# One index copy for four scatters in a graph network on one core

## The chip, the cores and the metric

The kernel runs on one core of a Trainium2 chip. The metric is device time in microseconds (us) of one execution, and lower is better. The five engines are TensorE (PE in the profile, with its weight loads as PEld), VectorE (DVE), ScalarE (ACT), GpSimd (POOL) and SyncE (SP). Each runs its own instructions in the order in which the program wrote them, and they wait for one another through semaphores.

## The reference

A graph of 12,500 nodes with 64 features and 200,000 edges, sorted by destination, goes through two blocks. The first block is a layernorm, a ReLU and two SAGE convolutions; the second is a layernorm, a ReLU and a message layer over the edges. Cut to what matters:

```python
def _sage_conv(x, src, dst, Wl, Wr, b):
    agg = jax.ops.segment_sum(x[src], dst, num_segments=N)
    cnt = jax.ops.segment_sum(jnp.ones((src.shape[0],), x.dtype), dst, num_segments=N)
    mean = agg / jnp.maximum(cnt, 1.0)[:, None]
    return mean @ Wl.T + b + x @ Wr.T
...
h = jnp.maximum(_layernorm(x, axis=-1), 0.0)
h = jax.nn.relu(_sage_conv(h, src, dst, W1l, W1r, b1))
x = x + _sage_conv(h, src, dst, W2l, W2r, b2)
h = jnp.maximum(_layernorm(x, axis=-1), 0.0)
inp = jnp.concatenate([h[src], h[dst], edge_attr_64], axis=-1)
msg = jax.nn.relu(inp @ W1 + b1) @ W2 + b2
x = x + _segment_mean(msg, src, N)
```

The part of `inp @ W1` that belongs to `edge_attr_64` needs neither convolution. The kernel calls its 200,000 rows of 64 the edge terms, and works them out early.

## The kernel before, in words

The nodes are cut into 49 blocks of 256. A cell is a pair of a source block and a destination block. There are 49 x 49 = 2401 cells, and each cell has 128 slots for its edges. Gathers and sums over edges are matmuls with one-hot matrices, cell by cell, so that edges have to be brought into the order of cells and slots.

**The sort.** The generator `sort(B)` handles the edges whose destination lies in block B: at most 34 columns of 128 edges. Among other things it works out, for each of them, the row that it has in a table in memory, and writes these rows as integers into `pos[:, B]`, a tile of 128 x 40 x 34 for the blocks below `EARLY` = 40 (line 651). The last nine blocks have theirs in `pos_late`. The operations of the sort (lines 589 to 666) are spread over the first convolution.

**The convolutions.** `some_cells` gathers four cells at a time (line 896, into PSUM tiles `got`), ScalarE copies them out (line 900), VectorE makes the one-hot matrix `hot` (line 750), and three turns later TensorE adds the cells up with it (line 775). The one-hot matrices of the gather, `turned` (line 741), are made by VectorE from source rows that SyncE loads (line 731). The main loop (lines 947 to 961) goes over all cells in groups of four, for layer 0 and then for layer 1. In each turn it emits `some_cells`, in layer 0 some steps of the sort and of the clearing of the tables, one half of the next `turned`, and then the work beside.

**The work beside.** `edge_terms` is a generator, and `Beside.passed` lets it go one step for every 4.45 units of due time, where a cell counts 1.1 in layer 0 and 0.9 in layer 1. For each group of four blocks it goes through their 17 pairs of columns, three at a time. A unit is one pair of columns of four neighbouring blocks. TensorE transposes the four (line 399), ScalarE copies them (line 405), TensorE multiplies them by the weights (line 414), and ScalarE copies the result into `terms_o`, which has three buffers (line 422). Then `scatter` sends the unit's 4 x 2 pieces of 128 rows to their places in memory, each by an indirect DMA that GpSimd issues. There are 170 such units in the convolutions, so 1360 scatters. The last nine blocks follow in the message stage with units of three and 306 scatters.

**One scatter.** For each half h of the pair and each block of the unit, VectorE copies one column of `pos` (128 rows by one integer) into a small tile `turn_i` of its own, of which there are 16 buffers (lines 380 and 381). GpSimd then issues the DMA that reads its 128 row numbers from that tile (line 382). After each scatter the generator yields. Of a unit's eight scatters, six go out one by one in the next unit's steps, and the rest at the end of those steps. A buffer of `turn_i` can be written again when the DMA that read from it has landed. GpSimd's scatters take eight DMA semaphores in turn.

**The order.** The program is emitted by hand in this order; VectorE's queue holds the copies between `hot`, `turned` and the operations of the sort. The messages come after both convolutions and read the edge terms back (line 1130).

Of the kernel before, what the change touches and what calls it, by code (L numbers as in the profile page):

```python
# [11 lines left out]
I32 = mybir.dt.int32  # L12
# [3 lines left out]
P = 128  # L16
# [98 lines left out]
def fast_path(  # L115
# [19 lines left out]
    nc = tc.nc  # L135
# [27 lines left out]
    EARLY = J * BJ * HALVES  # L163
# [7 lines left out]
    def table_of(B):  # L171

        if B < EARLY:
            q, i = divmod(B // J, BJ)
            return q * J + B % J, BJ, i
        i, j = divmod(B - EARLY, LJ)
        return HALVES * J + j, len(range(j, LATE, LJ)), i
# [78 lines left out]
    for n, b in enumerate((b1, b2, lb1, lb2)):  # L256
        t = consts.tile([P, D], FT, name=f"bias{n}")
# [97 lines left out]
    def edge_terms(work, psum, groups, ITEMS, U):  # L355


        loads = []
        for blocks in groups:
            step = ITEMS // len(blocks)  # L360
            loads += [(blocks, t0, min(step, TG - t0)) for t0 in range(0, TG, step)]

        def load(blocks, t0, m):
            n = len(blocks)
            e = work.tile([P, ITEMS, 2 * D], FT, name="edges")
            for i, B in enumerate(blocks):
                s = nc.sync.value_load(begin_i[0:1, B:B + 1], min_val=0, max_val=E - WIN)
                a = edge[bass.ds(s, WIN)].rearrange("(p t) d -> p t d", t=T)
                nc.sync.dma_start(e[:, i * m:(i + 1) * m].rearrange("p c d -> p (c d)"),
                                  a[:, 2 * t0:2 * (t0 + m)].rearrange("p t d -> p (t d)"))  # L370
            return e

        def scatter(o, unit):
            for h in range(2):
                for c, (B, tg, _) in enumerate(unit):
                    assert sorted_blocks() > B
                    t = 2 * tg + h
                    j, n, _ = table_of(B)
                    assert j in cleared
                    at = work.tile([P, 1], I32, name="turn_i", bufs=16)  # L380
                    nc.vector.tensor_copy(at, pos_of(B)[:, t:t + 1])
                    nc.gpsimd.indirect_dma_start(  # L382
                        out=terms[j][:], out_offset=bass.IndirectOffsetOnAxis(ap=at, axis=0),
                        in_=o[:, c, h], in_offset=None,
                        bounds_check=S * NB * n - 1, oob_is_err=False)
                    yield


        before = iter(())
        ahead = load(*loads[0])  # L390
        for at, (blocks, t0, m) in enumerate(loads):
            e = ahead
            items = [(B, t0 + c, e[:, i * m + c]) for c in range(m) for i, B in enumerate(blocks)]
            units = [items[u:u + U] for u in range(0, len(items), U)]
            for u, unit in enumerate(units):
                k = len(unit)
                pt = psum.tile([P, 4, P], FT, name="pE")
                for c, (_, _, a) in enumerate(unit):
                    nc.tensor.transpose(pt[:, c], a, ident)  # L399
                if u == 0 and at + 1 < len(loads):  # L400
                    ahead = load(*loads[at + 1])
                next(before, None)
                yield
                et = work.tile([P, U, P], FT, name="edges_t", bufs=2 if U == 4 else 1)
                nc.scalar.copy(et[:, :k], pt[:, :k])
                next(before, None)
                yield
                next(before, None)
                if U == 4:
                    next(before, None)  # L410
                yield
                pm = psum.tile([P, 4, 2, D], FT, name="pE")
                for c in range(k):
                    nc.tensor.matmul(pm[:, c], et[:, c], we, start=True, stop=True)  # L414
                next(before, None)
                yield
                next(before, None)
                yield
                for _ in before:
                    pass  # L420
                o = work.tile([P, U, 2, D], FT, name="terms_o", bufs=3)
                nc.scalar.copy(o[:, :k], pm[:, :k])
                before = scatter(o, unit)
                yield
        for _ in before:
            pass
# [72 lines left out]
    pos = terms_work.tile([P, EARLY, T], I32, name="pos", bufs=1)  # L499

    def pos_of(B):
        return pos[:, B] if B < EARLY else pos_late[:, B - EARLY]
# [196 lines left out]
    def sorted_blocks():  # L699
        return sorted_to[0] // STEPS  # L700
# [106 lines left out]
    work = layers.enter_context(tc.tile_pool(name="layers", bufs=2))  # L807
# [169 lines left out]
    work = ctx.enter_context(tc.tile_pool(name="last", bufs=2))  # L977
# [450 lines left out]
```

## Time and profile before

| what | us |
|---|---|
| median of three runs | 3727.71 |
| lowest and highest of them | 3725.05, 3731.02 |
| the profiled execution's own time | 3723.96 |
| its span, from the first to the last instruction | 3722.1 |
| features, first sort, set-up | 0 to about 200 |
| first convolution | about 200 to 1290 |
| second convolution | about 1290 to 2300 |
| messages, with the late blocks' edge terms | about 2300 to 3400 |
| messages of the late blocks, end | about 3400 to 3722 |

The granted TensorE clock is 0.991 over the span. In the profile a group of instructions is named by its line, its engine, its operation and the tiles that it writes and reads; then come its count, its busy time, the mean time of one in ns, and the idle time of its engine just before, with what ended it. "L382 POOL DMA_INDIRECT terms<-terms_o,turn_i" is thus the scatter on GpSimd, and "L381 DVE COPY turn_i<-pos" the copy of one column. Busy time counts what is covered by at least one instruction of the engine. The chain is followed from the last instruction back to what released each step.

### The profile page before, as it was taken

The page shows a single profiled execution, that of the slowest core. Times are in us where ns is not written, and L with a number is a line of the kernel's source. Part 1 is how long each engine was busy: PE and PEld are TensorE (multiplying, and loading weights), DVE is VectorE, ACT ScalarE, POOL GpSimd, SP SyncE. Part 2 cuts the span into 40 slices and gives each one's busy share as a digit, 9 for nine tenths or more (in the row PEclk, how much of TensorE's full clock was granted, in tenths as well). Part 3 has the DMA queues.
Part 4 walks back from the last instruction along what each step waited for, and adds up shares of the span by engine and source line. Part 5 has one row for each costly group of instructions (what it writes and reads, how often), then busy time and mean ns, then how long its engine had stood idle before and what let it go on. Part 6 is the DMA issues. An engine that isn't in the chain of part 4 may idle for free.

```text
span 3722.1 us, 130679 instructions
## 1 busy us (share of the span) xinstructions
PE 3505.5 (94%) x51318; PEld 3423.2 (92%) x51318; DVE 3322.8 (89%) x7346; ACT 2568.7 (69%) x5875; POOL 2732.6 (73%) x2306
## 2 busy tenths in 40 slices
PE   1799999999999999999999998999999999998987
PEld 0799999999999999999999998899999999998887
DVE  7899999999999978888888887899999999998998
ACT  3466666666666667777777776688888888876665
POOL 4057787777778777777777774688888888996454
PEclk9999999999999999999999999999999999999999
DMA  6654555555454344444444444666666666666664
GB/s 209 247 169 148 159 153 157 156 157 156 137 166 151 116 129 141 136 136 144 136 131 140 139 132 131 227 215 203 217 214 212 203 216 210 208 196 193 196 213 138
DMA packets 413697, 635.90 MB, mean 171 GB/s; under 512 B 94131, under 2 KB 296247, under 8 KB 413070
## 3 DMA queue, kind: packets, MB, share of 16 engines
q1 hardware_dynamic: 353106, 572.87, 48.7%
q0 software_dynamic: 53312, 51.36, 4.6%
q8 instruction: 402, 6.59, 0.7%
q10 hardware_dynamic: 6652, 3.24, 0.4%
q14 instruction: 225, 1.84, 0.2%
HBM read 474.72 MB, written 155.83 MB: 169 GB/s over the span
## 4 chain that ended last, share of the span: by engine, by line
PE 75%; DVE 15%; DMA 4%; issue 3%; ACT 2%; POOL 1%; SPq 1%; DVEq 0%; POOLq 0%; ACTq 0%
PE acc L775 26%; PE got L896 17%; PE got L1077 11%; PE got L1078 6%; PE pE L414 4%; DVE hot L750 3%; DVE turned L741 2%; PE pE L399 2%; DVE hot_r L635 2%; PE pX L645 2%; DVE turned_d L741 1%; DMA terms_in<-terms 1%; PE acc L839 1%; PE got L1074 1%; PE pX L617 1%
## 5 line engine op out<-in xcount | busy, mean ns | idle before, releaser
L382 POOL DMA_INDIRECT terms<-terms_o,turn_i x1666 | 1937.7, 1163 | 663.3 <-issue 220.5
L900 ACT CAST rows<-got 128x384 bf16<-128x384 f32 x2402 | 1038.5, 487 | 592.3 <-PE got L896 577.7
L775 PEld LDWEIGHTS <-hot 128*128 128x128 bf16 x12006 | 1029.5, 98 | 19.0 <-issue 7.9
L775 PE MATMUL acc<-rows,hot 128*128 128x193 bf16 x9604 | 1006.0, 247 | 0.7 <-DVE hot L750 0.7
L1089 POOL TENSOR_TENSOR hidden<-hidden 128x512 f32<-128x512 f32 (+1 forms) x602 | 756.3, 1257 | 259.6 <-ACT hidden L1086 179.3
L896 PEld LDWEIGHTS <-turned 128*128 128x128 bf16 x9604 | 814.7, 98 | 67.4 <-issue 27.5
L750 DVE TENSOR_TENSOR hot<-dcol,local 128x1024 bf16<-128x1024 bf16 x1202 | 814.3, 682 | 4.1 <-PE acc L775 3.7
L741 DVE TENSOR_SCALAR turned<-srow,nid 128x2048 bf16<-128x2048 bf16 (+1 forms) x906 | 780.4, 875 | 21.1 <-issue 10.7
L1077 PE MATMUL got<-ta,turned 128*128 128x128 bf16 x3920 | 599.8, 220 | 7.3 <-DVE turned L741 7.3
L1077 PE MATMUL got<-tb,turned_d 128*128 128x128 bf16 x3920 | 600.7, 221 | 1.7 <-DVE turned_d L741 1.1
L1078 PE MATMUL got<-tb,turned_d 128*128 128x64 bf16 x3920 | 546.9, 193 | 0.0
L1078 PE MATMUL got<-ta,turned 128*128 128x64 bf16 x3920 | 546.5, 193 | 0.0
L896 PE MATMUL got<-ta,turned 128*128 128x192 bf16 x4802 | 499.7, 247 | 37.4 <-issue 24.8
L1097 ACT ACTIVATE hot_a<-every,scol 128x256 bf16<-128x256 bf16 x1200 | 507.0, 493 | 0.0
L896 PE MATMUL got<-tb,turned 128*128 128x192 bf16 x4802 | 494.1, 246 | 0.8 <-DVE turned L741 0.5
L1086 ACT ACTIVATE hidden<-y 128x512 f32<-128x512 f32 (+1 forms) x301 | 190.4, 632 | 293.5 <-DVE y L1083 169.5
L1077 PEld LDWEIGHTS <-turned 128*128 128x128 bf16 x3920 | 362.8, 98 | 8.2 <-issue 7.8
L1077 PEld LDWEIGHTS <-turned_d 128*128 128x128 bf16 x3920 | 360.2, 98 | 2.9 <-DVE turned_d L741 2.4
L1078 PEld LDWEIGHTS <-turned 128*128 128x128 bf16 x3920 | 359.5, 98 | 1.2
L1078 PEld LDWEIGHTS <-turned_d 128*128 128x128 bf16 x3920 | 359.9, 98 | 0.0
L741 DVE TENSOR_SCALAR turned_d<-drow,nid 128x2048 bf16<-128x2048 bf16 (+2 forms) x302 | 324.9, 1117 | 0.0
L1099 ACT ACTIVATE hot_a<-hot_a 128x1024 bf16<-128x1024 bf16 x300 | 317.2, 1057 | 9.5
(227 smaller groups left out, 5302.4 us busy)
## 6 DMA issues: line engine op xcount, KB each, us to landing
srow<-srow_b SPq DMA_DIRECT2D x300, 512.0 KB
srow<-srow_k SPq DMA_DIRECT2D x149, 512.0 KB
drow<-drow_k SPq DMA_DIRECT2D x149, 512.0 KB
terms_in<-terms SPq DMA_DIRECT2D x294, 160.0 KB
edges<-in_edge_attr_dram SPq DMA_DIRECT2D x200, 192.0 KB
terms<-tb SPq DMA_DIRECT2D x200, 160.0 KB
terms<-tb SPq DMA_DIRECT2D x48, 640.0 KB
terms<-terms_o,turn_i POOLq DMA_INDIRECT x1666
```

Of the source, the lines that this page charges most:

```text
L382: nc.gpsimd.indirect_dma_start(out=terms[j][:], out_offset=bass.IndirectOffsetOnAxis(ap=at, axis=0), in_=o[:, c, h], in_offset=None, bound ...
L741: nc.vector.tensor_scalar(o[:, h, :n * S], r[:, :n * S], nid[:, h:h + 1], None, op0=OP.is_equal)
L750: nc.vector.tensor_tensor(o[:, :n], cols.rearrange("p (g c) -> p g c", c=2).unsqueeze(2).to_broadcast([P, n, 2 * P, 2]), local.rearrange(" ...
L775: nc.tensor.matmul(self.acc[B][:, h, :W3], lt, r[:, c, 0:W3], start=k + h == 0, stop=k == row - 1 and h == 1, skip_group_check=True)
L896: nc.tensor.matmul(p[:, (i - c) * D3:(i - c + 1) * D3], t[:, h, (a - c0 + i) * S:(a - c0 + i + 1) * S], table[:, (a + i) % NB, h], start=h ...
L900: nc.scalar.copy(g[:, c:c + m, :D3], p[:, :m * D3].rearrange("p (c d) -> p c d", c=m))
L1077: nc.tensor.matmul(p[:, c], lt, rt[:, 0:2 * D], start=i == 0, stop=False, skip_group_check=True)
L1078: nc.tensor.matmul(p[:, c, 0:D], lt, rt[:, 2 * D:], start=False, stop=i == 3, skip_group_check=True)
L1086: nc.scalar.activation(w[:, :n, 0:D], y[:, :n], AF.Relu)
L1089: nc.gpsimd.tensor_sub(w[:, :n, (i + 1) * D:(i + 2) * D], w[:, :n, j], upper(w)[:, :n, j])
L1097: nc.scalar.activation(q[:, c - k], every, AF.Abs, scale=-1.0, bias=scol[:, scol_at[last] + a + c:scol_at[last] + a + c + 1])
L1099: nc.scalar.activation(q[:, :n - k], q[:, :n - k], AF.Relu, bias=1.0, scale=-2.0)
```

## The change

For blocks below 40, `scatter` makes one tile of 128 x 4 for each half of the unit, with four buffers, and fills it with one VectorE copy. The copy takes the same column of the four neighbouring blocks, so its source has a stride of 34 integers. It stands just before the first of the four scatters, and the four scatters each take one column of it. The late blocks keep one copy for each scatter. An assertion says that the unit's blocks are neighbours with the same pair of columns.

```diff
         def scatter(o, unit):
             for h in range(2):
-                for c, (B, tg, _) in enumerate(unit):
+                B0, t = unit[0][0], 2 * unit[0][1] + h
+                assert [(B, tg) for B, tg, _ in unit] == [(B0 + c, unit[0][1]) for c in range(len(unit))]
+                if B0 < EARLY:
+                    four = work.tile([P, len(unit)], I32, name="turn_i", bufs=4)
+                    nc.vector.tensor_copy(four, pos[:, B0:B0 + len(unit), t])
+                for c, (B, _, _) in enumerate(unit):
                     assert sorted_blocks() > B
-                    t = 2 * tg + h
                     j, n, _ = table_of(B)
                     assert j in cleared
-                    at = work.tile([P, 1], I32, name="turn_i", bufs=16)
-                    nc.vector.tensor_copy(at, pos_of(B)[:, t:t + 1])
+                    if B0 < EARLY:
+                        at = four[:, c:c + 1]
+                    else:
+                        at = work.tile([P, 1], I32, name="turn_i", bufs=16)
+                        nc.vector.tensor_copy(at, pos_of(B)[:, t:t + 1])
                     nc.gpsimd.indirect_dma_start(
                         out=terms[j][:], out_offset=bass.IndirectOffsetOnAxis(ap=at, axis=0),
                         in_=o[:, c, h], in_offset=None,
```

## The prediction

> **What bounds the kernel now.** I read the page's busy shares and chain first, then the busy time by stage, then the chain and the waits of each convolution alone, then the timeline around the copies. The page:
>
> ```profile
> PE 3505.5 (94%) x51318; PEld 3423.2 (92%) x51318; DVE 3322.8 (89%) x7346; ACT 2568.7 (69%) x5875; POOL 2732.6 (73%) x2306
> PE 75%; DVE 15%; DMA 4%; issue 3%; ACT 2%; POOL 1%; SPq 1%; DVEq 0%; POOLq 0%; ACTq 0%
> ```
>
> TensorE sets the time over three quarters of the chain, VectorE over 15%. Those 15% are not spread evenly. Busy time by stretch (window, length, busy us and instructions of PE, PEld, DVE, ACT and POOL, granted clock, DMA share, GB/s; the rows are the first convolution, the second, and the first part of the message stage):
>
> ```profile
> 200.00:1290.00 1090.00, 1048.16 (x12357) 1006.99 (x12356) 1020.61 (x2608) 696.65 (x1746) 846.13 (x685) 1.00 0.50 151
> 1290.00:2300.00 1010.00, 1008.60 (x11463) 996.41 (x11461) 843.71 (x2453) 727.82 (x1956) 752.38 (x676) 1.00 0.44 137
> 2400.00:3300.00 900.00, 899.17 (x16903) 896.43 (x16901) 842.52 (x1297) 725.72 (x1366) 805.01 (x678) 1.00 0.67 210
> ```
>
> In the second convolution TensorE is busy for 1008.6 of 1010 us; its chain, added up, is 1005.2 us TensorE and 1.1 us VectorE, and no index copy stands on it. Nothing taken from VectorE there can shorten it. In the first convolution the sort runs beside the gather, VectorE is busy for 1020.6 of 1090 us, and the chain's pieces add up to 679.7 us TensorE, 327.1 VectorE, 33.5 ScalarE, 23.4 DMA, 22.9 issue. Only here can the change pay.
>
> Who waits there (window 200 to 1290; total us, times, longest):
>
> ```profile
> POOL terms L382 <- DVE turn_i L381: 49.6, 121, 3.0
> ...
> PE pX L645 <- DVE hot_r L635: 11.3, 15, 1.9
> ...
> PE got L896 <- DVE turn_i L381: 8.2, 8, 2.2
> ...
> PE pX L598 <- DVE hot L594: 5.5, 5, 1.5
> ...
> PE pX L598 <- DVE turn_i L381: 4.0, 6, 1.2
> ```
>
> When TensorE waits for VectorE, it is for about 0.9 us at a time (29.0 us in 34 waits by the four lines of PE). A wait named after turn_i is one for an operation that ended beside a copy, since TensorE reads no index.
>
> **The copies removed.** The scatter helper makes 1360 copies of one column for blocks below 40 (692 start in the first convolution, 668 in the second) and 306 for the late blocks, which keep theirs. The row of the first convolution, and one stretch of the timeline (start, us):
>
> ```profile
> L381 DVE COPY turn_i<-pos 128x1 int32<-128x1 int32 x692 | 86.9, 146 | 0.0
> ```
>
> ```profile
> 408.87 0.19 DVE L650 SCALAR_TENSOR_TENSOR pos_f<-rank,kv 128x34 f32<-128x34 f32 x1
> 409.09 0.18 DVE L651 TENSOR_SCALAR pos<-pos_f 128x34 int32<-128x34 f32 x1
> 409.18 0.75 DVE L741 TENSOR_SCALAR turned<-srow,nid 128x2048 bf16<-128x2048 bf16 x1
> 409.85 0.21 DVE L381 COPY turn_i<-pos 128x1 int32<-128x1 int32 x2
> 409.97 0.68 DVE L750 TENSOR_TENSOR hot<-dcol,local 128x1024 bf16<-128x1024 bf16 x1
> 410.57 0.15 DVE L381 COPY turn_i<-pos 128x1 int32<-128x1 int32 x1
> 410.63 0.68 DVE L750 TENSOR_TENSOR hot<-dcol,local 128x1024 bf16<-128x1024 bf16 x1
> ```
>
> A copy lasts 146 ns but the next operation starts 0.06 us after it: neighbours overlap. From start to next start the 692 copies take 43.4 us, 63 ns each, and that is what the stream gains. So 146 ns would overstate it 2.3 times. Of those 43.4 us, 11.3 us stand on the chain of the first convolution (about 26%, near VectorE's own share of the chain, 30%).
>
> **The copy of four that is added.** The trace has none. Lower bound: 63 ns, a one-column copy. Upper: the 128x34 write of pos (line 651), whose next operation starts about 94 ns after it. Four columns against 34 lie near the lower end: 63 + 3/33 of 31 = 66 ns. On the chain 11.3 us become 11.3 x 66 / (4 x 63) = 3.0 us (4.2 by the upper bound): **8.3 us** less, 7.1 at worst. In the second convolution 668 copies become 167, some 31 us of VectorE's time, hidden beside TensorE's 1008.6; if TensorE were not full there, that would count as well.
>
> [...]
>
> **The wait that is added.** Every copy but the first 16 waits on one DMA semaphore: buffer n is free when scatter n-16 has landed. A tile of four is free when all four of its scatters have, and it is asked for at the first of the next four. So scatter n-13 must have landed, not n-16, and one copy waits on four semaphores. That is up to two more semaphore instructions in VectorE's queue:
>
> ```profile
> L841 DVEq EVENT_SEMAPHORE  x98: 21/21/21, 155.1 to 2312.3; - x98
> L1081 DVEq EVENT_SEMAPHORE  x541: 21/50/4106, 2333.5 to 3697.6; - x181
> ```
>
> They run while the operation before them is still busy, mostly 0.6 us or more (a hot or a turned), so I take nothing. Uncovered, a pair costs about 0.1 us (two of line 1081 start 98 ns apart): 173 groups x 0.26 on the chain x 0.1 = 4.5 us.
>
> What queues behind a copy that waits is the next hot, and behind that TensorE's accumulation (line 775). How near is that wait? GpSimd is nearly full (window 200 to 1290):
>
> ```profile
> L382 POOL DMA_INDIRECT terms<-terms_o,turn_i x685 | 846.7, 1236 | 355.4 <-DMA terms<-tb 120.6 <-issue 90.5 <-DVE turn_i L381 49.6
> ```
>
> 1236 ns and a regular 0.305 us between two scatters; from 360 to 1290 us only 31 of 590 waited longer than that. Its lag behind the copies grows from 4.6 us (median of the first hundred) to 15.0 (of the eighth). I took each landing as the last increment of the scatter's semaphore before the semaphore's reuse eight scatters later, 2.1 to 6.4 us after the start. Against these, the copy of four would have had to spare in the first convolution: median 9 us, 5% under 3.7, least 0.3 (at 998 us), and 3.6 to 7 in its last 55 us. So no stall as the timing stands. At 1304 to 1430 us 13 groups would stall, 18.4 us together, 3.5 at most. That is in the second convolution, where hot runs 5 us ahead of TensorE at 1300 us and some 31 ahead from 1400: covered. Uncovered, it would be up to 18 us.
>
> But a first convolution that runs x us faster brings its copies x us nearer to GpSimd's scatters, and GpSimd does not speed up. Some 5 us are to be had before the end's slack (3.6 to 7) is gone, and the dip near 860 to 1000 us (about 3 us) takes a little on the way. **Sum**: 8.3 off the chain, some 3 given back to that wait: 5 us. Ends: 8.3 off and nothing off.
>
> On the profiled execution's 3723.96 us (span 3722.1 and 1.9 around it) that gives 3719; against the median of the runs, 3727.71, it gives **3722.7**. What a measurement here can tell from no change is about 0.2%, 7.5 us; the forecast lies inside it.
>
> **Rivals.** *The whole gain comes through.* For it: TensorE's waits for VectorE are 0.9 us each, while a VectorE stretch of the chain (38 stretches, 4.6 copies each) loses only 0.2 us, so VectorE mostly stays last. Against it: GpSimd's lag. With ScalarE's, DMA's and issue's pieces counted as VectorE's too (407 us at the copies' 4.0%, three quarters of it) it is 12 us: 3716; by the chain alone 3719.4. I put 3718 for it and count it as faster.
>
> *GpSimd becomes the bound.* Place: scatters of the first convolution, through the shorter ring of index buffers. Scatters with no copy in their first 966 ns lasted 1291 ns on average, with one 1183, with two 1147. If the copies are what lets GpSimd in, going from 0.6 to 0.16 copies a scatter makes it about 1274: 38 ns x 685 = 26 us later by 1290, less the 4 us of slack: 22 us, 3750. It decides from about 6 ns a scatter (4 us over 685). Against it: a long VectorE operation explains both the long scatter and the missing copy, and removing copies leaves the long operations' total as it is.
>
> [...]
>
> *It does nothing*: the semaphore instructions (4.5 us) and the ring take all: 3727.7.
>
> **How the numbers follow.** Forecast, 2 to 7 us off: 0.36, its own range 3720 to 3726. Nothing: 0.11. Whole gain: 0.33. GpSimd: 0.20. So faster 0.33, within 0.2% 0.47, slower 0.20. The range goes from the 12 us of the first rival with 3 us of scatter between runs, 3713, to 3737, 9 us slower: GpSimd 13 us later at the end of the first convolution, less its 4 us of slack. That leaves out perhaps 5% below and 14% above.
>
> **What would show it.** Copies: 340 of 128x4 and 306 of one column; VectorE busy in 200 to 1290 down by some 30 us. Right: the second convolution keeps its length and the first loses about 5. The step on the ring: idle of VectorE before the copy, by a DMA, near the end of the first convolution and in the 130 us after it, and none on TensorE behind the latter. The step on scatters: mean within 10 ns of 1236. Wrong: a mean of 1260 or more, a first convolution over 1090, or a second one that changes.

## The result: slower by a seventh of a per cent, and the profile after

The changed kernel takes 3732.96 us (median of 20 runs, 3723.93 to 3739.97); the kernel before, in 20 runs, 3727.75 (3719.49 to 3734.19). The ratio is 1.0014, with a 95% interval from 1.0008 to 1.0020. So it is 5 us slower, where 5 us faster was forecast. The time lies inside the stated range, but on the other side of the kernel before. The profiled execution took 3731.2 us, with a span of 3729.3, 7.2 us more than that of before.

The page after, busy shares and chain:

```profile
PE 3502.5 (94%) x51318; PEld 3419.9 (92%) x51318; DVE 3270.4 (88%) x6326; ACT 2568.9 (69%) x5875; POOL 2750.9 (74%) x2306
PE 74%; DVE 13%; DMA 5%; issue 4%; POOL 2%; ACT 1%; SPq 1%; DVEq 0%; POOLq 0%; ACTq 0%
```

VectorE has its 1020 instructions fewer and 52 us less busy time. On the chain VectorE has lost 2 points; DMA and GpSimd have won one each. The two convolutions (same windows and columns as before; the first really ends near 1340 us, where the first gather of the second starts):

```profile
200.00:1290.00 1090.00, 1041.07 (x12232) 999.27 (x12230) 986.81 (x2066) 690.08 (x1731) 859.00 (x678) 0.99 0.49 150
1290.00:2300.00 1010.00, 1008.56 (x11466) 996.24 (x11464) 816.78 (x1951) 726.39 (x1949) 756.48 (x683) 1.00 0.43 135
```

In the first window VectorE is busy for 34 us less, and yet TensorE did 125 matmuls fewer in it: the work is later. GpSimd did 7 scatters fewer and was busy 13 us longer. The start of the same gather matmul, read off both traces, tells where the time went (us):

| gather matmul | before | after | difference |
|---|---|---|---|
| 300 | 189.6 | 188.9 | -0.7 |
| 1500 | 498.1 | 495.0 | -3.1 |
| 2400 | 730.1 | 731.0 | +0.9 |
| 3000 | 883.3 | 890.8 | +7.6 |
| 4200 | 1197.8 | 1203.5 | +5.7 |
| 4800, the end of the first convolution | 1338.3 | 1348.5 | +10.2 |
| 9600, the end of the second convolution | 2304.1 | 2314.6 | +10.5 |

In this pair of traces the change wins 2.4 us between 190 and 500 us, loses 13 between 500 and 1340, and is neutral in the second convolution; 3 us come back in the message stage. What VectorE waited for in the window 200 to 1290 after the change, where before no copy waited at all:

```profile
DVE ranks L632 <- ACT ranks L625: 30.9, 30, 2.3
DVE turn_i L379 <- DMA terms<-terms_o,turn_i: 26.1, 25, 3.4
```

One such wait in the chain (start, us, what; window 705 to 732):

```profile
707.21 0.29 DVE both L830
707.80 0.97 POOL terms L389
...
717.96 1.67 POOL terms L389
...
721.32 6.99 DMA terms<-terms_o,turn_i
728.60 0.60 DVE hot L757
```

Read it downwards. The chain leaves VectorE, runs through a row of scatters on GpSimd and the landing of one of them, and comes back to VectorE's `hot`, which had been queued behind a copy of four. In the window 200 to 1290 the chain's pieces add up to 50.9 us on GpSimd's scatters and 72.0 us on their DMAs; before, they were 2.8 and 11.9. And the scatters themselves (same window):

```profile
L389 POOL DMA_INDIRECT terms<-terms_o,turn_i x678 | 859.4, 1268 | 342.2 <-issue 162.8 <-DMA terms<-tb 119.5 <-DMA terms<-terms_o,turn_i 19.0
```

They last 1268 ns on average instead of 1236. Nothing in the change touches the scatter, except that its index stands in a column of four.

### The profile page after: what moved, and what is told of

The parts are those of the page before. It is cut to its first block, busy times and chain, and to the rows that moved or that the text cites. A ratio compares the mean times of both kernels' runs of the same rounds, so it can differ in the third digit from the quotient of the medians.

```text
span 3729.3 us, 129317 instructions
## 1 busy us (share of the span) xinstructions
PE 3502.5 (94%) x51318; PEld 3419.9 (92%) x51318; DVE 3270.4 (88%) x6326; ACT 2568.9 (69%) x5875; POOL 2750.9 (74%) x2306
## 4 chain that ended last, share of the span: by engine, by line
PE 74%; DVE 13%; DMA 5%; issue 4%; POOL 2%; ACT 1%; SPq 1%; DVEq 0%; POOLq 0%; ACTq 0%
PE acc L782 26%; PE got L903 17%; PE got L1084 11%; PE got L1085 6%; PE pE L421 4%; DMA terms<-terms_o,turn_i 2%; PE pE L406 2%; PE pX L652 2%; DVE turned L748 2%; DVE hot L757 2%; DVE hot_r L642 2%; DVE turned_d L748 1%; POOL terms L389 1%; PE got L1081 1%; PE acc L846 1%
## 5 line engine op out<-in xcount | busy, mean ns | idle before, releaser
L1096 POOL TENSOR_TENSOR hidden<-hidden 128x512 f32<-128x512 f32 (+1 forms) x602 | 756.1, 1256 | 255.9 <-ACT hidden L1093 174.3
```

The costliest lines, as they stand in the source:

```text
L1096: nc.gpsimd.tensor_sub(w[:, :n, (i + 1) * D:(i + 2) * D], w[:, :n, j], upper(w)[:, :n, j])
```

## The experiments

Three theories stood at the start. RING: the index tiles now come free in fours, so VectorE waits. GPSIMD: the scatters became slower and GpSimd is the bound. SEMAPHORES: the 672 added semaphore instructions cost. Ratios are to the kernel before on the same chip.

**A first set, not comparable.** On its chip the kernel before itself took 4267 us (3724 to 3728 elsewhere), so its four kernels say nothing about 5 us. The granted clock of these runs of before was 0.95 to 0.96.

`e1`: eight tiles of four instead of four.

```diff
-four = work.tile([P, len(unit)], I32, name="turn_i", bufs=4)
+four = work.tile([P, len(unit)], I32, name="turn_i", bufs=8)
```

> The changed kernel with eight tiles of four instead of four, so that a copy waits for scatter n-29 instead of n-13; 340 copies and 672 semaphore instructions as in the change. Theory RING (the shorter ring of index tiles makes VectorE wait for landings, 26 us in the first convolution): these waits go to zero, the chain there loses its pieces on GpSimd and DMA (123 us), and the time is 3719 to 3725, below the 3727.8 of before. Theory GPSIMD (scatters last longer because the removed copies were openings for GpSimd, 1268 ns on average against 1236, and it is the bound whatever the ring): the waits leave the copies and come back at ScalarE's write of terms_o, which has three buffers; the time stays at 3730 to 3734. Theory SEMAPHORES (the added semaphore instructions cost): no change from 3733.

`e2`: the kernel before with 13 buffers.

```diff
-at = work.tile([P, 1], I32, name="turn_i", bufs=16)
+at = work.tile([P, 1], I32, name="turn_i", bufs=13 if B < EARLY else 16)
```

> The kernel before, with its own copy for each scatter, and 13 buffers for them in the convolutions instead of 16: only the ring is shortened, to what the first copy of four sees. RING: copies wait for landings, 5 to 25 us of VectorE idle in the first convolution, and the time is 3731 to 3741. GPSIMD: all copies are there, so scatters last 1236 ns and the time is 3728. SEMAPHORES: none is added, 3728.

`e3`: the change with idle one-column copies.

```diff
 at = four[:, c:c + 1]
+if c:
+    spare = work.tile([P, 1], I32, name="spare_i", bufs=16)
+    nc.vector.tensor_copy(spare, pos[:, B, t:t + 1])
```

> The changed kernel, and beside the second, third and fourth scatter of each half a one-column copy into a tile that nobody reads: VectorE's stream is as long as before the change, the ring is that of the change. RING: the saving is undone and the waits stay, 3734 to 3742. GPSIMD: the openings are back, the mean scatter of the first convolution falls from 1268 to about 1236 ns and the time returns to 3726 to 3730. SEMAPHORES: 3734 to 3742 as RING, with no fewer waits than the change if it is the semaphores that are late.

`e4`: the kernel before with 28 buffers.

```diff
-at = work.tile([P, 1], I32, name="turn_i", bufs=16)
+at = work.tile([P, 1], I32, name="turn_i", bufs=28 if B < EARLY else 16)
```

> The kernel before with 28 buffers for its copies instead of 16. No copy waited before, so RING, GPSIMD and SEMAPHORES all expect 3726 to 3730; if it is faster than that by more than 2 us, sixteen were already too few.

Measured there: e1 1.0384 (1.0354 to 1.0415), e2 1.0002 (0.9973 to 1.0030), e3 1.0329 (1.0294 to 1.0365), e4 1.0008 (0.9988 to 1.0028). Both kernels with a copy of four lost over 3% there, with and without idle copies. No such loss appeared in any other run of the change, and its cause stays open: the clock there is 3 to 4% lower, the time of the kernel before 14% longer. For 28 buffers this is the only run; it agrees with sixteen having been enough.

**The same again, at the usual pace.**

`f1`: eight tiles of four, as e1.

> The same kernel as e1_four_ring8 (eight tiles of four, a copy waits for scatter n-29), taken again because the first convolutions of that call, of the kernel before too, ran at another pace than in the runs that the question is about. RING: no copy waits for a landing, the first convolution is as long as before the change or shorter, the time is 0.9977 to 0.9995 of before. GPSIMD: the wait comes back at ScalarE's write of terms_o, 1.0005 to 1.002. SEMAPHORES: 672 semaphore instructions as in the change, 1.001 to 1.002.

Measured: 0.9999 (0.9990 to 1.0008). What ScalarE and TensorE waited for in the first convolution:

```profile
ACT terms_o L429 <- DMA terms<-terms_o,turn_i: 14.2, 8, 4.5
...
PEld pE L406 <- ACT terms_o L429: 9.9, 5, 3.8
```

The copies no longer wait, and the loss of the change is gone. The gain does not come, though; the result lies between the forecasts of RING and GPSIMD. The wait has moved to the next buffer in line, `terms_o`, whose three buffers come free when the scatters of three units back have landed; the scatters last 1273 ns. (The execution that was profiled took 3731.0 us, 6 above the median of its kernel, so these waits may be longer than usual.) RING is right about which wait costs the 5 us, and GPSIMD about what stands behind it. SEMAPHORES falls: at the two to a copy of the change, 664 semaphore instructions are there (the first eight copies need none), and nothing is lost.

`f2`: the kernel before with 13 buffers, as e2.

> The same kernel as e2_before_ring13 (the kernel before with 13 buffers). RING: some copies wait for landings in the first convolution, 5 to 25 us, 1.0005 to 1.003 of before. GPSIMD and SEMAPHORES: 1.000.

Measured: 1.0005 (0.9996 to 1.0014), scatters 1245 ns. The trace has one wait of 0.3 us at a copy up to 1290 us, and eight between 1304 and 1350, 12.2 us together and 3.1 at most. The second convolution does not cover these: TensorE's first gather in it, near 1340 us, waits until VectorE has got past them. That wait before, and in f2:

```profile
PE got L896 <- DVE bad_t L965: 0.3, 1, 0.3
PE got L896 <- DVE bad_t L965: 4.5, 1, 4.5
```

`bad_t` names the operation with which VectorE ended just before the gather began. From gather matmul 4800 to 4900 f2 loses 5.5 us against the trace of before. So the shorter ring alone can cost 4 to 5 us at this one place. The time shows neither that it does as a rule nor that it does not: the interval reaches from 0.9996 to 1.0014. (f2 is also a little stricter than the change: each of its copies waits for the scatter 13 back, in the change only one in four.)

`f3`: the change with idle copies, as e3.

> The same kernel as e3_four_idle_copies (the change, with three one-column copies that nobody reads beside each copy of four). RING: 1.002 to 1.004 of before, copies wait as in the change or more. GPSIMD: mean scatter of the first convolution back to 1236 ns, 1.000. SEMAPHORES: 1.002 to 1.004.

Measured: 1.0000 (0.9991 to 1.0009). Its scatters in the first convolution:

```profile
L392 POOL DMA_INDIRECT terms<-terms_o,turn_i x686 | 847.7, 1236 | 354.8 <-issue 166.5 <-DMA terms<-tb 120.5 <-DMA terms<-terms_o,turn_i 18.5
```

With 1020 useless copies put back, the scatters last 1236 ns again, although their index still stands in a column of four; no copy waits with the short ring, and the loss is gone. RING alone expected 1.002 and more. So the loss of the change goes away with a longer ring (f1) and with faster scatters (f3): it is made by slower scatters and a ring too short to ride over them. What the ring costs without the slower scatters stays open (f2).

`f4`: one copy of eight columns for a unit, four tiles.

```diff
-if B0 < EARLY:
-    four = work.tile([P, len(unit)], I32, name="turn_i", bufs=4)
-    nc.vector.tensor_copy(four, pos[:, B0:B0 + len(unit), t])
+if B0 < EARLY and h == 0:
+    eight = work.tile([P, len(unit), 2], I32, name="turn_i", bufs=4)
+    nc.vector.tensor_copy(eight, pos[:, B0:B0 + len(unit), t:t + 2])
```

> One copy of eight columns (both halves) for a unit's eight scatters, with four tiles of eight: the copy waits for scatter n-25, and there are 170 copies with eight semaphores to wait for instead of 340 with four. RING: no waits at the copies, and another 12 us less in VectorE's stream: 0.997 to 0.9995 of before. GPSIMD: 1.0005 to 1.002. SEMAPHORES: the number of semaphore instructions stays near 672, 1.001 to 1.002.

Measured: 1.0042 (1.0028 to 1.0055), outside what all three expected. The first convolution:

```profile
ACT terms_o L429 <- DMA terms<-terms_o,turn_i: 36.7, 20, 6.2
...
PEld pE L406 <- ACT terms_o L429: 27.1, 17, 5.7
```

```profile
L389 POOL DMA_INDIRECT terms<-terms_o,turn_i x668 | 861.6, 1290 | 340.8 <-issue 177.6 <-DMA terms<-tb 125.9 <-DMA terms<-terms_o,turn_i 14.7
```

Fewer VectorE instructions still, slower scatters still, a longer wait at `terms_o`. No copy waits for more than 0.2 us up to 1290 us. So the slower scatters cost time with the ring out of the way too, through `terms_o`.

**Who paces whom.**

`g1`: the change with another pace of the edge terms.

```diff
-beside.passed((z - a) * (1.1, 0.9)[layer])
+beside.passed((z - a) * (1.06, 0.93)[layer])
```

> The changed kernel with the edge terms paced at 1.06 a cell in the first convolution and 0.93 in the second, instead of 1.1 and 0.9: scatters fall due every 1.61 us in the first instead of 1.55, and every 1.45 in the second instead of 1.50. OPENINGS (without the copies a scatter lasts 1.27 us and 0.305 follow, so GpSimd falls behind and is what the first convolution ends up waiting for): at 1.61 GpSimd keeps up, the waits at the copies fall from 26 us to under 5, and what the copies saved on VectorE shows: 0.997 to 0.999 of before. RING: waits fall as well, by less; 0.999 to 1.001. If neither holds and the copies of four cost something of their own: 1.001 as the change.

Measured: 0.9987 (0.9978 to 0.9996). No copy waits up to 1290 us, with scatters of 1288 ns, but one waits for 2.7 us at 1330, just before the first gather of the second convolution, and TensorE with it:

```profile
PE got L903 <- DVE bad_t L972: 1.7, 1, 1.7
```

`g2`: the kernel before with that pace.

> The kernel before with the same pace, 1.06 and 0.93. OPENINGS and RING: no copy waited before, so nothing is won, 0.9990 to 1.0005; GpSimd's lag no longer grows in the first convolution. If the pace by itself pays (fewer matmuls and copies of the edge terms in the crowded convolution), 0.997 to 0.999, and the gain of g1_four_pace is not the change's.

Measured: 0.9989 (0.9980 to 0.9998). The pace pays by itself, so g1's gain is not the change's; with GpSimd given 4% more time, change and kernel before are equal within the noise. In the traces g1 is 2.7 us ahead of g2 at gather matmul 4800 and 0.5 us behind at 4900, across that one wait. So even here the ring takes the gain back; OPENINGS, which expected it to show, missed that.

`g3`: as f3, with memsets for idle operations.

```diff
-nc.vector.tensor_copy(spare, pos[:, B, t:t + 1])
+nc.vector.memset(spare, 0)
```

> As f3_four_idle_copies, but the three idle operations beside each copy of four are memsets of 128x1, which read nothing. OPENINGS, if any short operation lets GpSimd in: the first 300 scatters last 1.21 to 1.24 us as with idle copies, against 1.27 to 1.31 without, and the time is 1.000. If a copy's reading or its longer pass is what counts: 1.26 us and more, 1.001 to 1.002.

Measured: 0.9977 (0.9968 to 0.9986), faster than the kernel before. Scatters of the first convolution:

```profile
L392 POOL DMA_INDIRECT terms<-terms_o,turn_i x695 | 825.2, 1187 | 376.2 <-issue 171.3 <-DMA terms<-tb 120.2 <-DMA terms<-terms_o,turn_i 21.6
```

The scatters are 81 ns shorter than after the change, by operations that do nothing. That beats the expectation, which was 1.000. No copy waits in this trace. The memsets add little to VectorE's stream (some 8 ns each in h1 below), so it is the scatters that took the waits away, and not a VectorE that comes later.

`g4`: the kernel before with every copy made twice.

```diff
 nc.vector.tensor_copy(at, pos_of(B)[:, t:t + 1])
+if B < EARLY:
+    spare = work.tile([P, 1], I32, name="spare_i", bufs=4)
+    nc.vector.tensor_copy(spare, pos[:, B, t:t + 1])
```

> The kernel before with a second, idle copy beside each of the 1360 copies: the dose the other way. OPENINGS: scatters of the first convolution fall from 1236 ns to about 1180 to 1210, and GpSimd's lag there no longer grows; VectorE's stream is 43 us longer there, of which 11 stand on the chain, so 1.001 to 1.004. If scatters last as long as VectorE is busy and copies play no part: 1236 ns or more, 1.003 to 1.006.

Measured: 1.0063 (1.0049 to 1.0077), scatters 1277 ns instead of the 1180 to 1210 of the theory. So "each copy is an opening for GpSimd" is too simple: one copy in a place shortens scatters (f3: 1268 to 1236 ns), two in the same place lengthen them (1236 to 1277). The other theory on record, that scatters last as long as VectorE is busy, expected 1236 ns or more and 1.003 to 1.006 and comes near; but after the change VectorE is busy for less and the scatters last longer, which contradicts it.

**The disputed cost by itself.**

`h1`: scatters beside VectorE in thirteen rhythms.

```python
for name in SECTIONS:
    ...
    for k in range(K):
        nc.gpsimd.indirect_dma_start(
            out=table[:], out_offset=bass.IndirectOffsetOnAxis(ap=at[:, k:k + 1], axis=0),
            in_=rows, in_offset=None, bounds_check=P * K - 1, oob_is_err=False)
    ...
    for n in range(150):
        if kind == "hot" or kind == "mix" and n % 3:
            hot()
        else:
            turned()
        for m in more:
            small[m]()
```

> Nothing of the network is computed; the output holds x. Thirteen stretches, in each 40 scatters of 128 rows beside VectorE, which is idle, or runs hot alone, turned alone, or two hots and one turned in turn, plain or with one short operation after each: a copy of 128x1, two of them, a memset of 128x1, a copy of 128x4 from columns 34 apart. [...] If short operations play no part: all stretches beside hot alike within 20 ns.

Measured, by stretch (40 scatters each; busy us, mean ns):

```profile
L81 POOL DMA_INDIRECT terms_mix<-terms_o,turn_i x40 | 71.3, 1784 | 58.1 <-DMA terms_mix<-terms_o,turn_i 56.4 <-DVE turn_i L79 1.8
...
L81 POOL DMA_INDIRECT terms_hot_copy_copy<-terms_o,turn_i x40 | 56.1, 1402 | 58.7 <-DMA terms_hot_copy_copy<-terms_o,turn_i 56.9 <-DVE turn_i L79 1.8
L81 POOL DMA_INDIRECT terms_mix_four<-terms_o,turn_i x40 | 52.3, 1308 | 58.1 <-DMA terms_mix_four<-terms_o,turn_i 56.4 <-DVE turn_i L79 1.8
L81 POOL DMA_INDIRECT terms_mix_copy<-terms_o,turn_i x40 | 49.4, 1234 | 60.5 <-DMA terms_mix_copy<-terms_o,turn_i 55.8 <-issue 2.9 <-DVE turn_i L79 1.8
...
L81 POOL DMA_INDIRECT terms_hot_copy<-terms_o,turn_i x40 | 47.4, 1185 | 59.1 <-DMA terms_hot_copy<-terms_o,turn_i 57.3 <-DVE turn_i L79 1.8
L81 POOL DMA_INDIRECT terms_mix_memset<-terms_o,turn_i x40 | 44.5, 1112 | 58.5 <-DMA terms_mix_memset<-terms_o,turn_i 56.8 <-DVE turn_i L79 1.8
L81 POOL DMA_INDIRECT terms_hot_memset<-terms_o,turn_i x40 | 41.0, 1026 | 60.4 <-DMA terms_hot_memset<-terms_o,turn_i 55.7 <-issue 2.9 <-DVE turn_i L79 1.8
L81 POOL DMA_INDIRECT terms_hot<-terms_o,turn_i x40 | 39.4, 986 | 58.9 <-DMA terms_hot<-terms_o,turn_i 57.1 <-DVE turn_i L79 1.8
L81 POOL DMA_INDIRECT terms_idle<-terms_o,turn_i x40 | 38.9, 974 | 87.8 <-DMA terms_idle<-terms_o,turn_i 84.8 <-DVE turn_i L79 2.9
```

In the plain mixture 14 of the 40 scatters came after VectorE's 150 operations were over and took 970 ns each; the 26 beside them took 2222. In the other stretches two or three of the 40 came so late. The other four: turned alone 1217, with a copy 1417, with a memset 1221; hot with a copy of four 1232. So VectorE's short operations do decide, but with both signs. Beside like operations a copy lengthens the scatter (986 to 1185, 1217 to 1417, two of them to 1402). Beside a mixture of hot and turned it shortens it by 550 ns, a copy of four by less (476), and a memset by most (672); with only the scatters beside operations counted, the 2222 fall to 1256, 1326 and 1120. By OPENINGS a short operation lets GpSimd in; half of it falls, for the scatters get shorter beside the mixture and longer beside like operations. That all stretches beside hot would be alike within 20 ns falls too: they go from 986 to 1402. Hot alone hardly lengthens a scatter (974 to 986), though it keeps VectorE full (0.0 us idle before the 1150 hots of all stretches). The timeline shows a scatter beside the plain mixture (start, us; window 1010 to 1018):

```profile
1013.19 0.74 DVE L61 TENSOR_SCALAR turned<-srow,nid 128x2048 bf16<-128x2048 bf16 x1
1013.70 2.29 POOL L81 DMA_INDIRECT terms_mix<-terms_o,turn_i  x1 [1.44 <-DMA terms_mix<-terms_o,turn_i]
1013.86 1.28 DVE L55 TENSOR_TENSOR hot<-dcol,local 128x1024 bf16<-128x1024 bf16 x2
1015.06 0.74 DVE L61 TENSOR_SCALAR turned<-srow,nid 128x2048 bf16<-128x2048 bf16 x1
1015.72 1.28 DVE L55 TENSOR_TENSOR hot<-dcol,local 128x1024 bf16<-128x1024 bf16 x2
```

It starts while a turned runs, goes on past two hots and the next turned, and ends at 1015.99, 0.19 us after that turned's end at 1015.80. Such ends, 0.12 to 0.19 us after a long operation, are the rule in the stretches with turned or copies: 35 to 38 of the 40 scatters, and 24 of the 26 in the plain mixture, but only 11 with a memset in the mixture. This fits a scatter that is held until such an operation is over, and in the plain mixture over several. It is argued and not shown: beside hot alone, where most scatters take 969 ns, nearly the 974 beside an idle VectorE, the ends are as regular, 0.24 us after a hot.

**Is the gain the change's?**

`h2`: the change with eight tiles, idle memsets and the pace of g1, three edits shown above (the memsets with four spare tiles instead of sixteen).

> The change with eight tiles of four, idle memsets of 128x1 beside the second, third and fourth scatter, and the pace 1.06 and 0.93. If the gains of g1 (0.9987) and g3 (0.9977) add up: 0.996 to 0.9975 of before. If both only relieve the same GpSimd: 0.9975 to 0.9985.

Measured: 0.9963 (0.9950 to 0.9977), 3714.6 us against 3726.4 of the kernel before: the fastest of all. Scatters last 1172 ns, no copy waits for a landing. Of this gain the pace alone gave 0.9989 (g2); the rest is 0.26%.

`h3`: the kernel before with a memset beside each copy.

```diff
 nc.vector.tensor_copy(at, pos_of(B)[:, t:t + 1])
+if B < EARLY:
+    spare = work.tile([P, 1], I32, name="spare_i", bufs=4)
+    nc.vector.memset(spare, 0)
```

> The kernel before with an idle memset of 128x1 beside each of the 1360 copies. If the memset is what lets GpSimd in, scatters of the first convolution fall from 1236 ns to 1190 to 1215; VectorE gets 1360 operations of some 60 ns more, so its chain grows by about 11 us: 1.000 to 1.003 of before, and the gain of g3 is the copies saved and GpSimd relieved together. If the gain of g3 is the memsets' alone: 0.997 to 0.999.

Measured: 1.0004 (0.9995 to 1.0013), scatters 1178 ns, a little under the 1190 to 1215 expected. Faster scatters by memsets win the kernel before nothing; the 340 memsets that it has more than g3 come to some 3 us of VectorE's stream, as an estimate from h1's 8 ns each. So g3's gain is most likely the copies saved, once GpSimd keeps up. No run shows the saving apart from the memsets.

`h4`: the change again.

> The changed kernel as it is, beside the others on one chip. 1.0008 to 1.002 of before as first measured; mean scatter of the first convolution 1260 to 1290 ns, copies waiting for landings 15 us or more there.

Measured: 1.0015 (1.0006 to 1.0024). The two rows that matter came back, and the wait of f2 and g1 came with them:

```profile
DVE turn_i L379 <- DMA terms<-terms_o,turn_i: 24.4, 20, 3.6
PE got L903 <- DVE bad_t L972: 3.3, 1, 3.3
```

```profile
L389 POOL DMA_INDIRECT terms<-terms_o,turn_i x681 | 858.7, 1261 | 343.8 <-issue 155.7 <-DMA terms<-tb 120.7 <-DMA terms<-terms_o,turn_i 21.8
```

This second trace of the change differs in detail from the first. Against the trace of before it is 1.6 us ahead at gather matmul 1500, 5.6 behind at 4800 and 10.2 behind at 4900: the sum is as before, but 4.6 us of the loss fall on the first gather of the second convolution.

All of them together (mean scatter, and waits of the copies for landings, in the trace from 200 to 1290 us; TensorE's wait at the first gather of the second convolution, named after `bad_t`):

| kernel | ratio, interval | scatter ns | copies' waits us | first gather us |
|---|---|---|---|---|
| the change | 1.0014, 1.0008 to 1.0020 | 1268 | 26.1 | 0.3 |
| h4, the change again | 1.0015, 1.0006 to 1.0024 | 1261 | 24.4 | 3.3 |
| f1, ring of eight | 0.9999, 0.9990 to 1.0008 | 1273 | none; terms_o 14.2 | 0.3 |
| f2, before, ring 13 | 1.0005, 0.9996 to 1.0014 | 1245 | 0.3 | 4.5 |
| f3, idle copies | 1.0000, 0.9991 to 1.0009 | 1236 | none | 0.3 |
| f4, copy of eight | 1.0042, 1.0028 to 1.0055 | 1290 | 0.6; terms_o 36.7 | 0.3 |
| g1, pace | 0.9987, 0.9978 to 0.9996 | 1288 | none | 1.7 |
| g2, before, pace | 0.9989, 0.9980 to 0.9998 | 1244 | none | none |
| g3, idle memsets | 0.9977, 0.9968 to 0.9986 | 1187 | none | 0.3 |
| g4, before, two copies | 1.0063, 1.0049 to 1.0077 | 1277 | 1.6; terms_o 5.5 | 1.7 |
| h2, ring, memsets, pace | 0.9963, 0.9950 to 0.9977 | 1172 | none | none |
| h3, before, memsets | 1.0004, 0.9995 to 1.0013 | 1178 | none | 0.3 |

## Why the prediction was wrong, point by point

*What bounds the kernel.* Right. From matmul 4800 to 9600 the second convolution takes 965.9 us before and 966.1 after, with 27 us less of VectorE.

*The copies removed and the copy of four.* Right in kind, a little off in size. 172 copies of four take 74 ns each from start to next start, where 66 was taken and 63 to 94 allowed; the first convolution's stream of copies falls from 43.4 to 12.7 us, by the 30 us forecast. Part of the gain is seen in the first 500 us, 2.4 of the 8.3 that the whole convolution was to give. Two pairs of kernels in which no copy waits agree with all of it: g3 against h3 (0.9977 against 1.0004, with scatters of 1187 and 1178 ns) and h2 against g2 (0.9963 against 0.9989) differ by 0.27 and 0.26%, some 10 us. Both changed kernels have idle memsets, though, so this is an inference and no measurement of the saving alone.

*The semaphore instructions.* Right: two to a copy, as the row shows, and no loss in f3, which has them too.

```profile
L379 DVEq EVENT_SEMAPHORE  x672: 21/35/50, 231.6 to 2279.1; - x168
L379 DVE COPY turn_i<-pos x340: 149/167/398, 207.3 to 2279.9; 128x4 int32<-128x4 int32 x170
```

*The ring.* The place, the scatter n-13 and the small slack (0.3 to 7 us) were right. The cover behind 1304 us was only half right: in the profiled execution nine stalls of up to 3.9 us between 1315 and 1423 us left TensorE waiting for 0.3 us, but in h4 its first gather of the second convolution waited for 3.3 us, and for 4.5 in f2. The forecast took the hots' lead over TensorE as cover and put everything behind 1304 us into the second convolution; its first gather, near 1340, has no such lead. Nor was the hots' lead the 31 us of the forecast: in the trace of before a hot ended 3.0 to 7.0 us, at the median 5.1, before the matmul that reads it started, for the hots that ended between 1290 and 1440 us. The term of the sum was mis-sized too: "some 3 given back to that wait" became 26 us of waits, and in this trace the convolution lost 13 us from 500 us on, the copies' saving already taken off.

*The step that failed* is the one under it: "GpSimd does not speed up". It was taken that GpSimd's pace would stay as it was and only VectorE come nearer to it. GpSimd slowed down. The first 300 scatters took 473.4 us before and 484.0 after, 10.6 us more, which is more than the 4 to 7 us of slack. Of the 26 us that VectorE waited, 19 come after that, and from there both kernels' scatters went at one pace (629.7 and 629.2 us for the next 400).

*The rival that came true* is the second, GpSimd as the bound through the shorter ring, which had 0.20. Its scatter was forecast at 1274 ns and measured at 1268 and 1261. (The 966 ns of its reckoning are the shortest scatter in the trace of before; the mean is 1236 in the first convolution and 1114 in the second.) That it came so near is partly luck: the same reckoning, each copy an opening, expected 1180 to 1210 ns of g4, where 1277 were measured. The argument against it failed, that "removing copies leaves the long operations' total as it is": in h1 VectorE is full beside hot alone, the plain mixture and the mixture with memsets, and the scatters last 987, 2222 and 1120 ns beside them. It matters which operations they are and what stands between them. Its price, 22 us, was too high. GpSimd's first 300 scatters lost 10.6 us, and after that the waits stopped the drift; what VectorE saved came off it.

*The gain coming through whole* was the first rival's; f1 shows that even with no ring in the way nothing comes; the wait next in line is that at `terms_o`.

What stays open: what holds a scatter, and why a copy has one sign beside a mixture and the other beside like operations. In h1 a scatter waits for a landing before it starts (56.4 us in all before the 40 of the plain mixture), so its phase against VectorE repeats: the one shown starts 0.51 us after a turned's start, its neighbours 0.49 and 0.50. In the kernel before only 0.305 us lie between most scatters, its phases are others, and the numbers of h1 are not to be carried over as they stand.

## What to carry to other kernels

Before instructions are taken out of one engine, look at who runs beside it with no slack: here GpSimd was behind its copies all through the first convolution from the 200th scatter on, by 1.1 to 14.6 us, and the trace showed no wait at a copy with sixteen buffers; with thirteen (f2) there are nine. A tile made of four old ones came free here with the last of its four readers: with four such tiles the copies waited for 26.1 us in the first convolution, with eight (f1) not at all. So give it the depth in readers, not in bytes. And price a removed instruction by what the neighbours do without it as well: put idle ones back in its place and see whether the time returns.

## What the hardware showed that was not expected

A 128x1 memset on VectorE that nobody needs made the kernel faster: 1020 of them took the change from 1.0014 to 0.9977 of the kernel before. A memset lasts 59 ns, but in h1 it starts beside a long operation (0.02 us after a hot's start in the mixture with memsets), and a hot with its memset takes 612 ns from start to start where a hot alone takes 604: it adds little to the stream. A scatter's time on GpSimd went from 974 ns beside an idle VectorE to 1784 beside a plain mixture of two kinds of operations (2222 for those that ran wholly or partly beside it), and hot alone, as busy as the mixture, left it at 986.
